# Moving six pairs' leftover gate/up rows into the attention stage of an adaLN transformer block, with a two-step layernorm

## The chip, the cores and the metric

The kernel is one launch on one core of a Trainium2 chip. It is measured in microseconds of device time for one execution; of several executions the median is given. TensorE (PE in the profile) multiplies matrices, PEld is its loading of stationary operands, VectorE (DVE), ScalarE (ACT) and GpSimd (POOL) work element by element, SyncE (SP) issues most of the DMAs. A profile is one execution that the hardware profiler recorded.

## The reference

An adaLN block in float32: x has 2 batches of 1024 tokens of width 1024. All matrices are dense.

```python
mod = (_silu(L0_c) @ L0_wmod).reshape(2, 6, 1, -1)
sa, ca, ga, sb, cb, gb = (mod[:, i] for i in range(6))
ga, gb = (sign * max(|g|, 0.25) for g in (ga, gb))
h = _layernorm(x) * (1 + ca) + sa
# attention: qkv = clip(h @ Wqkv.T); layernorm of q and of k over the width of 1024;
# 32 heads of 32, causal, ALiBi slopes, softmax, then the output product with Wout
x = x + ga * attention(h)
h = _layernorm(x) * (1 + cb) + sb
# gated MLP with 2752 inner rows
x = x + gb * (((_silu((h @ Wg.T) * ag) * ((h @ Wu.T) * au)) @ Wd.T) * ad)
```

## The kernel before

**Products.** Every large product is done by the Strassen-Winograd scheme: seven products of quarter operands in place of eight. `seven` runs them for 256 tokens (a *pair* of token tiles; `j` counts four pairs of each batch `b`) with two alternating PSUM banks x and y, four matmuls of 512 columns each; a float32 matmul shows as two records in the profile. `operand` builds the seven stationary operands of a pair from the attention's result, after it has fetched the reciprocals of the softmax sums (`rb`, spread over partitions) and multiplied them in (`aoA`).

**Order.** The stages are: modulation vectors; the q, k and v projections of batch 0; attention of batch 0 beside the projections of batch 1; attention of batch 1 beside the output products of six pairs (all four of batch 0, two of batch 1); a tail; the gate and up products of the FFN (line 1789, tiles gx, gy, ux, uy); the down product.

**Attention.** A unit is four heads (`k` counts eight groups), 512 queries and 128 keys: `scores` writes two PSUM tiles `sc`, each with one buffer; ScalarE writes exponentials into `p` (line 1056, 4 instructions of up to 512 columns; for k = 0 and 1 in pieces of 128 and 256 columns); GpSimd cuts the causal triangle; two units later `weigh` multiplies by v into `av`. Sums of `p` are added by VectorE and GpSimd and summed over keys by `settle`; `reciprocals` sends the sums of one (batch, 512 queries) through DRAM and back. TensorE's order is fixed as the program has it (`in_order`); other engines' orders are made by the framework from its own estimates, with each engine working in order.

**The dealing out.** `attention` and `dense_work` are generators that yield estimated microseconds. `together` advances the dense one until its sum reaches `share(a)`, where `a` is attention's sum. Each unit gives `unit_us` twice, once after its scores and once after its weighing. `DENSE0` and `DENSE1` are how much dense work is laid beside batch 0 and batch 1:

```python
def unit_us(b, qb, k, jb):
    return (0.2 + width(qb, jb) / 512) * SLOW[b].get(k, 1.0)
...
    return LEAD + DENSE0 + DENSE1 * max(a - att_us[0] - 8.0, 0.0) / (att_us[1] - 8.0)
```

**The output step of a pair** (`output`): seven products in chunks of two matmuls; `read` copies P1, U2 and P5 to SBUF (ScalarE) and adds the others to them (VectorE), multiplies by the gate and adds to the residual tile `xr` (GpSimd). Then the residual goes to DRAM, and `normalize` makes the second layernorm: statistics on VectorE, Ln and Exp on ScalarE, a correction and the product on VectorE. Four *turns* (four transposes each, evacuated by VectorE into `h2t`) follow as entries of a `Todo` list; `places` lets one entry run between chunks of the next pair. During attention a Todo entry has one spare PSUM bank (`banks.others`), which `settle` uses too.

**The rest rows.** The inner rows of the FFN are taken in five blocks of 512; 192 rows are left over. `rest_rows` computes them for a pair: three row products (gate rows, up rows, and 64 of each), each 8 matmuls of 256 columns (16 records `rest<-hl,restw`), then Silu on ScalarE, a product on VectorE and two DMA stores (`actr`). All eight pairs are done in the tail, as cover for other things there: `with_turns` lays rows beside turns, `between` lays them beside the output products of the last two pairs. Their weights (`rest_weights`, 1.5 MB) are loaded at the start of the tail. `fetch` brings h2 of a finished pair back (`hl`); `second` forms the Strassen combinations of both batches (`inner_b`, tiles `inner_T`, `oo`) and stores them (`bop`) for the FFN.

Of the kernel before, what the change touches and what calls it, by code (L numbers as in the profile page):

```python
# [12 lines left out]
FP = mybir.dt.float32  # L13
# [467 lines left out]
def kernel(  # L481
# [225 lines left out]

    def normalize(tiles, outs, small, nm):

# [8 lines left out]
        ve = small.tile([P, n], FP, tag="ve", name=f"ve_{nm}")  # L718
        nc.vector.tensor_scalar_add(ve, mv[:, :, 1], EPS)
        lv = small.tile([P, n], FP, tag="lv", name=f"lv_{nm}")  # L720
        nc.scalar.activation(lv, mv[:, :, 1], AF.Ln, bias=eps_t)
        rstd = small.tile([P, n], FP, tag="rstd", name=f"rstd_{nm}")
        nc.scalar.activation(rstd, lv, AF.Exp, scale=-0.5)
        fix = small.tile([P, n], FP, tag="fix", name=f"fix_{nm}")
        nc.vector.tensor_mul(fix, rstd, rstd)
        nc.vector.tensor_mul(fix, fix, ve)
        nc.vector.tensor_scalar(fix, fix, -0.5, 1.5, ALU.mult, ALU.add)
        nc.vector.tensor_mul(rstd, rstd, fix)
        for m, (t, o) in enumerate(zip(tiles, outs)):
            nc.vector.tensor_scalar(o, t, mv[:, m, 0:1], rstd[:, m : m + 1], ALU.subtract, ALU.mult)  # L730
# [5 lines left out]
    SLOW = ({0: 1.6, 1: 1.2}, {0: 2.6, 1: 1.4})  # L736
# [121 lines left out]
    class Todo:  # L858


        def __init__(self, banks):
            self.banks, self.list = banks, []
# [4 lines left out]
        def run(self, n, all_=False):  # L867
            for _ in range(min(n, len(self.list))):
                if not all_ and not self.banks.fresh():
                    return  # L870
                self.list.pop(0)(self.banks.turn())
                yield TURN

        def places(self, q0, n, side=lambda e: None):
# [3 lines left out]
            def between(q):  # L878
                side(order.index(q))
                if order.index(q) >= q0:  # L880
                    yield from self.run(n)
# [3 lines left out]
    def tokens(b, j, todo, ap_, xp, sm):  # L885
# [7 lines left out]
        normalize(xs, xs, sm, f"x{b}_{j}")  # L893
# [16 lines left out]
    def projections(b, pools, banks, places, extra=None, other=None, side=lambda n, e: None):  # L910
# [8 lines left out]
        for part in range(3):  # L919
            bt = weights_b(wp_, wqkv_t[:, ts(part, D)], f"{b}_{part}", wt_dram[part], other, b == 0 and part == 1)  # L920
            for j in range(NT // 2):
# [43 lines left out]
                normalize(raws, raws, sm, f"qk{b}_{part}_{j}")  # L965
# [15 lines left out]
    def behind(ins, first):  # L981

        tc.add_manual_dep(
            ins.ins, first.ins.name,
            mybir.DependencyInfo(mybir.DependencyClass.NoSync, mybir.DependencyReason.DATA),
            reason="behind",
        )

# [5 lines left out]
    def unit_us(b, qb, k, jb):  # L994
        return (0.2 + width(qb, jb) / 512) * SLOW[b].get(k, 1.0)
# [1021 lines left out]
```

## Time and profile before

| | us |
|---|---|
| three runs | 2932.33, 2937.59, 2945.91 |
| median | 2937.59 |
| the profiled execution | 2934.67 |
| its span, first to last instruction | 2932.9 |
| TensorE busy in it | 2728.3 |
| VectorE, ScalarE, GpSimd busy | 1436.5, 685.7, 1287.2 |
| attention of batch 1, first scores to last weighing | 989.4 to 1408.7 |
| first gate product of the FFN | 1585.45 |

Times in the profile count from the start of the span. A line of the timeline has the start, the length, the engine, the source line, the operation, what it writes and reads, and in brackets how long the engine had been idle and who released it. The granted clock of TensorE is a share of full speed. A line `L745` or `L748` is the helper that records all matmuls or transposes of the attention and output stages, so the tiles' names tell them apart.

### The profile page before, as it was taken

The page shows a single profiled execution, that of the slowest core. Times are in us where ns is not written, and L with a number is a line of the kernel's source. Part 1 is how long each engine was busy: PE and PEld are TensorE (multiplying, and loading weights), DVE is VectorE, ACT ScalarE, POOL GpSimd, SP SyncE. Part 2 cuts the span into 40 slices and gives each one's busy share as a digit, 9 for nine tenths or more (in the row PEclk, how much of TensorE's full clock was granted, in tenths as well). Part 3 has the DMA queues.
Part 4 walks back from the last instruction along what each step waited for, and adds up shares of the span by engine and source line. Part 5 has one row for each costly group of instructions (what it writes and reads, how often), then busy time and mean ns, then how long its engine had stood idle before and what let it go on. Part 6 is the DMA issues. An engine that isn't in the chain of part 4 may idle for free. (4 is left out here: it accounts for less than half of the span.)

```text
span 2932.9 us, 29881 instructions
## 1 busy us (share of the span) xinstructions
PE 2728.3 (93%) x10271; PEld 1335.4 (46%) x10271; DVE 1436.5 (49%) x2285; ACT 685.7 (23%) x1523; POOL 1287.2 (44%) x1270
## 2 busy tenths in 40 slices
PE   6999997899999888888799999999999998999998
PEld 2444332333333222222456444444444446888776
DVE  5666522466553455655554444453534446434442
ACT  1322242354434455555111011010101100000000
POOL 3312145434353655555456546463644641222343
PEclk9999998999999989999899999999999999999999
DMA  9867787463642654432578658575765759554542
GB/s 339 301 253 286 291 276 234 146 215 109 223 146 77 211 155 157 141 107 96 159 232 275 223 172 287 159 273 180 241 217 173 256 154 300 153 163 136 163 144 80
DMA packets 377571, 579.12 MB, mean 197 GB/s; under 512 B 21590, under 2 KB 278712, under 8 KB 366276
## 3 DMA queue, kind: packets, MB, share of 16 engines
q1 hardware_dynamic: 359768, 554.54, 58.1%
q10 hardware_dynamic: 17644, 22.59, 2.4%
q8 instruction: 84, 1.38, 0.2%
q14 instruction: 75, 0.61, 0.1%
HBM read 411.89 MB, written 165.17 MB: 197 GB/s over the span
## 5 line engine op out<-in xcount | busy, mean ns | idle before, releaser
L1056 ACT ACTIVATE p<-sc,kw 128x128 f32<-128x128 f32 (+3 forms) x1024 | 421.4, 513 | 356.6 <-PE sc L745 337.5
L745 PE MATMUL bank<-wT,a 128*128 128x512 f32 x768 | 361.5, 614 | 14.0 <-DVE raw L951 7.2
L1088 POOL TENSOR_TENSOR p<-p,p 128x1024 f32<-128x1024 f32 (+3 forms) x128 | 262.7, 2052 | 237.9 <-PE av L745 210.6
L1088 DVE TENSOR_TENSOR p<-p,p 128x1024 f32<-128x1024 f32 (+3 forms) x192 | 242.3, 1274 | 186.8 <-POOL p L1060 143.4
L745 PE MATMUL bank<-wB,a 128*128 128x512 f32 x576 | 265.9, 606 | 1.7 <-DVE raw L949 1.3
L745 PE MATMUL sc<-cq,ck 32*128 32x512 f32 (+3 forms) x1536 | 199.7, 558 | 69.2 <-ACT p L1056 68.8
L745 PEld LDWEIGHTS bank<-wT,a 128*128 128x128 f32 x768 | 142.6, 195 | 202.1 <-issue 181.0
L1060 POOL TENSOR_SCALAR_AFFINE_SELECT p<-p 128x256 f32<-128x256 f32 x256 | 136.4, 545 | 144.1 <-ACT p L1056 141.7
L745 PE MATMUL av<-p,cv 128*32 128x512 f32 (+3 forms) x1536 | 173.7, 515 | 20.7 <-POOL p L1060 20.7
L745 PEld LDWEIGHTS bank<-wB,a 128*128 128x128 f32 x576 | 105.2, 191 | 147.7 <-issue 129.1
L745 PEld LDWEIGHTS sc<-cq,ck 32*128 32x128 f32 x1536 | 66.8, 191 | 203.3 <-ACT p L1056 119.9
L1789 PE MATMUL gy<-bt,sig 128*128 128x512 f32 x280 | 132.5, 595 | 10.4 <-DMA bt<-bop_B 5.6
L1789 PE MATMUL gx<-bt,sig 128*128 128x512 f32 x280 | 131.6, 592 | 0.0
L1789 PE MATMUL ux<-bt,siu 128*128 128x512 f32 x280 | 131.6, 592 | 0.0
L1789 PE MATMUL uy<-bt,siu 128*128 128x512 f32 x280 | 131.6, 592 | 0.0
L745 PEld LDWEIGHTS av<-p,cv 128*32 128x32 f32 x1536 | 33.9, 110 | 139.7 <-issue 84.9
L951 DVE TENSOR_TENSOR raw<-P,bank 128x512 f32<-128x512 f32 x48 | 32.8, 684 | 125.3 <-PE bank L745 116.8
L1789 PEld LDWEIGHTS gy<-bt,sig 128*128 128x128 f32 x280 | 52.4, 190 | 80.8 <-issue 71.0
L1789 PEld LDWEIGHTS uy<-bt,siu 128*128 128x128 f32 x280 | 53.2, 190 | 67.0 <-issue 65.8
L1789 PEld LDWEIGHTS ux<-bt,siu 128*128 128x128 f32 x280 | 53.2, 190 | 67.0 <-issue 65.1
L1789 PEld LDWEIGHTS gx<-bt,sig 128*128 128x128 f32 x280 | 53.2, 190 | 67.0 <-issue 65.9
L745 PE MATMUL rest<-hl,restw 128*128 128x256 f32 x288 | 67.0, 391 | 14.9 <-DVE xn L730 14.9
(416 smaller groups left out, 4500.1 us busy)
## 6 DMA issues: line engine op xcount, KB each, us to landing
bt<-bop_T SPq DMA_DIRECT2D x140, 512.0 KB
bt<-bop_B SPq DMA_DIRECT2D x99, 512.0 KB
a<-hop SPq DMA_DIRECT2D x20, 1792.0 KB
wm<-in_L_wmod_dram SPq DMA_DIRECT2D x48, 512.0 KB
wB<-in_L_attn_Wqkv_dram SPq DMA_DIRECT2D x21, 1024.0 KB
aq_S<-act_S SPq DMA_DIRECT2D x16, 1280.0 KB
qk<-qs SPq DMA_DIRECT2D x16, 1024.0 KB
act_S<-asS SPq DMA_DIRECT2D x30, 512.0 KB
```

The source lines that it names most:

```text
L745: return in_order(nc.tensor.matmul(*args, **kw_))
L951: nc.vector.tensor_add(dst, part_t[MATE[q]], bank)
L1056: nc.scalar.activation(p[:, g, lo:hi], sp[:, g, lo:hi], AF.Exp, bias=kw[:, d, h_ : h_ + 1])
L1060: nc.gpsimd.affine_select(out=p[:, :, 0:P], in_=p[:, :, 0:P], pattern=[[0, 2], [1, P]], compare_op=ALU.is_ge, fill=0.0, base=0, channel_mu ...
L1088: adders[b](half, jb).tensor_add(dst, dst, ps[half][:, :, 0:n])
L1789: nc.tensor.matmul(ps.rearrange("p (j t) -> p j t", j=NJ), ins[mat][qa][:, c2, :], bt[:, :, c2, :], start=(q in ("P1", "P2", "P5") and c2 ...
```

## The change

**Rest rows.** `rest_rows` is replaced by `rest_piece`, one row product as a Todo entry. `output` adds three of them after the turns of each pair while attention runs, so six pairs (all of batch 0 and two of batch 1) have their rows dealt out beside attention. Their weights are loaded when the output stage begins. Silu is written as x times the reciprocal of 1 + exp(-x): Identity and Exp on ScalarE, minimum, reciprocal and product on VectorE. Pairs 2 and 3 of batch 1 keep their rows in the tail.

**Layernorm.** `normalize` makes the statistics at once and returns the rest as a function. For the projections of batch 1 and the output steps up to pair 0 of batch 1 it is run at the first place of the next step (`Todo.first`, `Todo.place`); elsewhere at once. The Ln is put behind the last exponential recorded before it.

**Dealing out.** `unit_us` is half of an estimate of the exponentials' time less a part for the products; `DENSE1` goes from 136 to 205.

**The tail.** Both operands of the last two pairs are made at once (one in its own pool); the tail's fetches go to SP's queue; the output products of the last two pairs run without rows between them. `xr` has two buffers instead of four, and the sums are kept in the copies' tiles.

```diff
-    SLOW = ({0: 1.6, 1: 1.2}, {0: 2.6, 1: 1.4})
     def unit_us(b, qb, k, jb):
-        return (0.2 + width(qb, jb) / 512) * SLOW[b].get(k, 1.0)
+        n, span, end = width(qb, jb), SPAN.get(k, QB), (qb + 1) * QB
+        y0 = end - n
+        parts = [y + span - max(y, y0) for y in range(y0 // span * span, end, span)]
+        return 0.5 * (0.4 + sum(1.2 + 4 * 0.39 * w / 512 for w in parts) - (0.25 + 0.8 * n / 512))
-    LEAD, DENSE0, DENSE1 = 16.0, 370.0, 136.0
+    LEAD, DENSE0, DENSE1 = 16.0, 370.0, 205.0
     def normalize(tiles, outs, small, nm):
...
+        def rest_():
...
+            ln = nc.scalar.activation(lv, mv[:, :, 1], AF.Ln, bias=eps_t)
+            if last_exp[0] is not None:
+                behind(ln, last_exp[0])
...
+        return rest_
     class Todo:
...
+        def first(self, go, now):
+            if now:
+                go()
+            else:
+                assert self.due is None
+                self.due = go
+        def place(self):
+            if self.due is not None:
+                self.due()
+                self.due = None
         def run(self, n, all_=False):
+            self.place()
             for _ in range(min(n, len(self.list))):
                 if not all_ and not self.banks.fresh():
                     return
-                self.list.pop(0)(self.banks.turn())
-                yield TURN
+                more = self.list.pop(0)(self.banks.turn())
+                if more is None:
+                    yield TURN
+                else:
+                    yield from more
     def projections(...)
-                normalize(raws, raws, sm, f"qk{b}_{part}_{j}")
+                todo.first(normalize(raws, raws, sm, f"qk{b}_{part}_{j}"), b == 0)
     def output(...)
-            normalize(xs, xn, sm, f"f{b}_{j}")
+            todo.first(normalize(xs, xn, sm, f"f{b}_{j}"), b == 1 and j >= NJ // 2 - 1)
...
+            if rest is not None:
+                for r in range(3):
+                    todo.add(rest_piece(b, j, r, *rest))
+    def rest_piece(b, j, r, rest_w, pool):
...
+        def go(bank):
+            hl = kept[b, j].rearrange("p k h t -> p k (h t)")
+            ps = bank[:, 0:256]
+            for k in range(KC):
+                matmul(ps, rest_w[r][:, k, :], hl[:, k, :], start=(k == 0), stop=(k == KC - 1))
+            if r != 1:
+                g, e = tile_("rg", r), tile_("re", r)
+                nc.scalar.activation(g[hi], ps[lo], AF.Identity, scale=ag_)
+                nc.scalar.activation(e[hi], g[hi], AF.Exp, scale=-1.0)
+                nc.vector.tensor_scalar(e[hi], e[hi], FAR, 1.0, ALU.min, ALU.add)
+                nc.vector.reciprocal(e[hi], e[hi])
+                nc.vector.tensor_mul(g[hi], g[hi], e[hi])
+                sig[b, j, gate] = g
+            if r != 0:
+                ac = tile_("rac", r)
+                nc.vector.scalar_tensor_tensor(ac[hi], ps[hi], au_, sig[b, j, gate][hi], ALU.mult, ALU.mult)
+                nc.sync.dma_start(
+                    rest_dram[gate][0 : n1 if gate else P, b, j], ac[hi].rearrange("p (h t) -> p h t", h=2)
+                )
+            yield 3.5
+        return go
     # output stage
-            for n, k in (("oga", 1), ("tok", 4), ("opart", 1), ("osmall", 2), ("ao", 1))
+            for n, k in (("oga", 1), ("tok", 2), ("opart", 1), ("osmall", 2), ("ao", 1))
+        rest = rest_weights(rwp, nc.sync), rwp
     # tail
-    fetch(0, 0, nc.scalar)
-    rest_w = rest_weights(rest_pool, nc.scalar)
-    fetch(1, 0, nc.scalar)
-    made = {(1, NJ // 2): operand(1, NJ // 2, opools[1])}
-    fetch(0, 1)
-    with_turns(rows((0, 0), (1, 0)))
-    fetch(1, 1)
-    def between():
-        yield from rows((0, 1))
-        second(0)
-        yield from rows((1, 1))
-    together(
-        between(), output(1, range(NJ // 2, NJ), *out_args, made, 3), lambda a: 0.6 * OUT_US / 2 * a / 20.6
-    )
+    made = {(1, NJ // 2): operand(1, NJ // 2, opools[1], wide)}
+    made[1, NJ // 2 + 1] = operand(1, NJ // 2 + 1, opools[1])
+    fetch(0, 0)
+    fetch(1, 0)
+    alone(todo.run(len(todo.list), True))
+    fetch(0, 1)
+    fetch(1, 1)
+    second(0)
+    alone(output(1, range(NJ // 2, NJ), *out_args[:-1], None, made, 3))
     in_range(rest_pool, rps)
+    second(1)
     fetch(0, 2)
-    second(1)
     fetch(0, 3)
-    with_turns(rows((0, 2), (1, 2)))
+    with_turns(rows(2))
     second(2)
-    alone(rows((0, 3), (1, 3)))
+    alone(rows(3))
```

## Prediction before the result

> **What bounds the kernel now.** I read the page's slices first, then the windows by stage, then the waits and the timeline around the change.
>
> ```profile
> PE   6999997899999888888799999999999998999998
> ACT  1322242354434455555111011010101100000000
> PEclk9999998999999989999899999999999999999999
> ```
>
> A slice is 73 us. TensorE (PE) is busy almost everywhere; the weak stretch is slices 13 to 19, attention of the second batch (8 tenths, where ScalarE is at 4 to 5) and the end of it. Nothing here is bound by ScalarE's sum of work. The windows, with the borders I took from the attention's tiles, give it in microseconds (columns: stretch, length, busy time of PE, its weight loads, VectorE, ScalarE, GpSimd, then granted clock, DMA share, GB/s):
>
> ```profile
> 600.00:800.00 200.00, 197.52 (x917) 74.70 (x916) 124.86 (x217) 90.74 (x233) 80.81 (x60) 1.00 0.51 177
> 989.00:1410.00 421.00, 350.62 (x2026) 113.04 (x2024) 232.87 (x343) 227.89 (x553) 242.50 (x231) 0.91 0.40 124
> 1410.00:1425.00 15.00, 14.05 (x40) 5.92 (x40) 5.85 (x11) 1.02 (x2) 4.90 (x5) 1.00 0.80 271
> 1425.00:1440.00 15.00, 0.25 (x1) 0.00 (x0) 7.12 (x19) 0.86 (x3) 5.39 (x4) 0.62 0.81 239
> 1440.00:1540.00 100.00, 96.10 (x337) 62.66 (x338) 56.44 (x99) 12.43 (x20) 47.26 (x41) 0.97 0.72 210
> 1540.00:1585.00 45.00, 43.32 (x208) 37.55 (x207) 24.23 (x52) 8.45 (x12) 18.06 (x18) 1.00 0.83 283
> 1585.00:1634.00 49.00, 46.45 (x109) 20.22 (x108) 21.23 (x30) 5.62 (x10) 46.02 (x63) 1.00 0.77 244
> ```
>
> Attention of batch 0 (600 to 800) leaves PE no gap. Attention of batch 1 (989 to 1410) leaves 70.4 us idle in 421, and runs at a mean clock of 0.91. Then 15 us finish the dealt-out output products, 15 us are empty, and from 1440 on the tail is full. So there is room before 1410 and none after 1440: that is what this change trades on. Who makes the 70 us (waits, 989 to 1410):
>
> ```profile
> PE sc L745 <- ACT p L1056: 55.1, 43, 7.1
> ACT lv_f L721 <- DVE mv_f L717: 28.5, 4, 8.9
> PE bank L748 <- DVE h2t L851: 9.4, 2, 7.6
> ```
>
> Scores wait for the exponentials that still read the one score buffer. Some exponentials are late only because a layernorm's Ln stands in front of them in ScalarE's order and waits for VectorE's statistics. The timeline shows it: scores at 1264.20, Ln at 1272.37, the exponentials right behind it, the next scores after 6.16 us of idle PE.
>
> ```profile
> 1264.20 0.71 PE L745 MATMUL sc<-cq,ck 32*128 32x256 f32 x8
> 1272.37 0.30 ACT L721 ACTIVATE lv_f<-mv_f,eps_t 128x2 f32<-128x2 f32 x1 [8.90 <-DVE mv_f L717]
> 1272.57 1.55 ACT L1056 ACTIVATE p<-sc,kw 128x256 f32<-128x256 f32 x4
> 1274.17 0.81 PE L745 MATMUL sc<-cq,ck 32*128 32x128 f32 x8 [6.16 <-ACT p L1056]
> ```
>
> The end of attention, and what the rows cost:
>
> ```profile
> 1431.17 0.32 SPq L1218 DMA_DIRECT2D rb<-rec  x1
> 1434.66 3.37 ACTq L1342 DMA_DIRECT2D restw<-in_L_ffn_Wg_dram  x1
> 1440.13 13.36 PE L745 MATMUL rest<-hl,restw 128*128 128x256 f32 x48 [14.89 <-DVE xn L730]
> 1448.23 1.27 POOL L1233 TENSOR_TENSOR aoA<-aoA,rb 128x512 f32<-128x512 f32 x1 [12.34 <-DMA rb<-rec]
> 1563.83 10.53 PE L745 MATMUL rest<-hl,restw 128*128 128x256 f32 x48
> 1585.45 1.88 PE L1789 MATMUL gx<-bt,wgA 128*128 128x512 f32 x4
> ```
>
> 48 records of one pair take 10.4 us warm, so one of its three row products is 3.45 us.
>
> **The tail.** From 1425 to the first FFN product at 1585.45 are 160.4 us. PE's work in it: 24 row products x 3.45 = 82.8; two output steps, 112 records x 0.43 (3.60 us for eight with their ramp) = 48.2; twelve turns (0.60 each plus about 0.3 until the evacuation) = 10.8; sum 141.8; so 18.6 are waits, 14.9 of them the gap before 1440.
> The change moves 15 row products into attention; the three of pair (1,1) stay behind it as the last of the list, six more belong to the last two pairs. PE's work falls by 51.8 to 90. The cover falls with it, so the waits must be counted anew:
> - Operand of the third pair. Last weighing 1408.72, sum stored 1413.36, read back 1420.64, reciprocal 1424.08, stored 1425.06, fetched from 1431.17, product with it at 1448.23: 39.5 us. The legs to 1431 stay. The last leg, 17.1 us, shared the DMA with 1.5 MB of row weights, which now come long before; bounds are 3.4 us (the reload at 1420.64) and 17.1, and I take 9, since 2 MB of `hl` still travel. With the multiply that is T+33, T being the last weighing. PE has the settling, four turns and three row products until T+17: 16 us idle (10 to 24).
> - Last normalization: 1540.1 to 1550.2 now, less two table loads of 1.28, so 7.5; the first row product hides 3.45: 4 us. The last turn's evacuation before `rows(3)`: 2 us.
> - Combinations (`second`): without rows between them VectorE's `inner` writes stand in front of evacuations of the two output steps, and can wait for a store (6.83 us seen at 1569); two banks give 3.4 us of slack. 0 to 14, I take 5.
> Sum 90 + 16 + 4 + 2 + 5 = 117, against 160.4: 43 us less. On SP's queue the moved steps cost nothing that I count: the actr stores (two a pair) now go out during attention (DMA share 0.40). With two buffers instead of four an xr load waits for the normalization that moved one product later, and chunk loads stand behind it; but chunks are fetched two groups, some 30 us, ahead, and the first product that needs xr ends about 16 us into its step. Were that cover gone, each of six steps would lose up to the 10 us of a normalization.
>
> The trace's own row for that fetch (17.1 us with row weights issued from ScalarE's queue) already says that another queue did not shield it. The Trainium skill, DMA: Bandwidth & Descriptors, section Issuing engines are not separate DMA queues, gives the rule: all queues share the same 16 engines and interleave. By the rule the fetches moved from ScalarE's queue to SP gain nothing by that, and only the earlier time of the row weights can; a sum with no gain on this leg would leave 8 us more idle.
>
> **Attention of batch 1.** Before, dealt work was out at 1425: 350.6 busy + 70.4 idle + 15 after = 436 us from 989. After:
> - Busy: 350.6 + 14.0 (the work of 1410 to 1425) + 15 x 3.45 = 416.4.
> - Clock: four records took 3.78 us at 1206.26 against 1.98 elsewhere. Scores and weighing of batch 1 sum to 195.5 us, of batch 0, the same products at clock near 1, to 178.0; 270 output records cost 0.526 each against 0.470 there. All of it is 32 us; denser work recovers a part, I take 10 (0 to 32).
> - Idle of layernorm: longest waits of 7.6, 7.1, 6.2 and 3.8, in all 24.7. The Ln is now put behind the last exponential and one product later; its statistics are ready by then (3 us of GpSimd, 0.9 us of VectorE against a step of some 4 us). 4 remain (0 to 15).
> - Other idle, 45.7: short gaps of a microsecond between units. `unit_us` now gives a full unit 2 x 1.06 x 205/234 = 1.85 us of dense work, one chunk of four records, and a 128-wide unit 1.35 (0.51 before), so gaps of narrow units are filled; a row product of 3.45 is too long for one gap. 27 remain (15 to 46).
> - New: the row products use the only spare bank. It is held through Identity and Exp (0.47 each, as the Silu of this shape), on VectorE min-add and product (0.44 each, by `inner` of this shape), reciprocal (0.94 for 128 wide, so 1.87) and the last product 0.48: 4.2 us, up to 7 behind an addition of 1.5 and its neighbour. Until the next taker PE has a chunk and a unit's products, 4 us. So 0 to 3 us for ten of fifteen, 0 to 30; I take 8. PE being in order, scores stand behind it. VectorE's 32 us more (5 x 6.4) on 233 of 421 and ScalarE's 9.4 on 228 are hidden.
> Sum 416.4 - 10 + 4 + 27 + 8 = 445, so T = 1434: 9 us later. Bounds: -26 (unlikely all together) and +70.
>
> The clock term by a page: the Trainium skill, TensorE: Matmul & The Clock Gate, section What's actually happening, halves the clock after an idle window of about 3.4 us and restores it after as long a busy one. This speaks against the tail of the change: its 16 us gap starts the third output step cold, an estimated 1.7 us by that page, which I leave out of the sum.
>
> **Batch 0** is full of PE work; its eight normalizations delay ScalarE by 2.7 to 5.5 us each without PE showing it, while the Ln one product later can make a turn wait. I take 0 (-8 to +8).
>
> **Transfers.** DMA share times length from 1410 to 1634 is 171 us. Without row weights and with what now falls into attention some 150 remain, in about 167 us: 0.9 of full use, near the best stretches (0.83). I add 4.
>
> Sum: -43 + 9 + 0 + 4 = -30. The profiled execution took 2934.67 (span 2932.9), so 2904.7; the median lies 2.9 above it: **2908**.
>
> **Rivals.**
> 1. Better: clock recovers wholly and rows fit the gaps; T 15 earlier than 1425: 2880. For it: batch 0 with as many dense records holds 1.00. Against: gaps are short. 0.15.
> 2. Transfers bind the tail: if 0.8 is all it can hold, 150 us of transfers need 188, 20 more than I allow: 2926. For it: 6.8 to 14.7 us waits on stores after 1550. Against: 0.83 over 45 us. 0.15.
> 3. Slower, by the one spare bank: each of ten row products makes PE wait 3 us (30), no gap is filled (46), the clock stays: 416.4 + 30 + 46 + 4 = 496, T 60 later, net +21: 2959. Without the bank it is a shift of 30; it turns slower by over 0.5% once the wait passes 2.4 us each. For it: VectorE's queue holds additions of 0.9 to 1.5 us. Against: at least a chunk stands between. 0.18.
> That the rows are not dealt out in time is covered by the third: they would then drain behind attention, uncovered.
>
> **Numbers.** 0.5% (14.7 us) is about what a measurement of this kernel can tell from no change. My case has 0.52 and its own range of 2886 to 2926. Faster: 0.52 and 0.15, less an edge, 0.66; same 0.17; slower 0.17. The range reaches over the first rival's price and to the third's: 2872 to 2958.
>
> **What would show it.** Right: last weighing near 1434, clock above 0.95 and PE idle near 40 in batch 1; no Ln wait over 3 us there; an idle stretch of 10 to 24 us before output step (1,2); first gx about 117 us after the last weighing. Wrong: PE waiting for VectorE before row products (rival 3), or for bt or gate weights at the first FFN products (rival 2).

## The result and the profile after

The changed kernel takes 2970.84 us (median of four runs, 2965.85 to 2978.29) against 2939.15 for the kernel before, run beside it: a ratio of 1.011, interval 1.0078 to 1.0142. It is slower by some 32 us, where 31 less were forecast. Its profiled execution took 2970.97 us (span 2969.2) against 2934.67 (span 2932.9). The stages, by positions in the two timelines:

| stage, us | before | after | difference | forecast |
|---|---|---|---|---|
| up to the first scores of batch 1 | 989.4 | 985.1 | -4 | 0 |
| from there until the dealt-out work is done | 435.6 (to 1425) | 485.7 (to 1470.8) | +50 | +9 |
| from there to the first gate product | 160.4 | 124.5 | -36 | -43 |
| from there to the FFN's second group (first `gx<-bt,wgS`) | 51.4 | 77.6 | +26 | 0 (and 4 for transfers) |
| the rest | 1296.1 | 1296.3 | 0 | 0 |

The slices of the page after, as they were shown of before:

```profile
PE   7999897999997898888876899999999998999998
ACT  1322143344443445445300101010110101000000
PEclk9999999999998899999888999999999999999999
```

Counted from 0 as in the prediction, slices 13 to 18 of PE (attention of batch 1) are about as weak as before. Slices 19 to 21 (the end of attention, the tail and the FFN's first products) stand at 7, 6 and 8 tenths, where it was 7, 9 and 9, and the granted clock dips in the same three. The windows, same columns as before (stretch, length, busy time of PE, weight loads, VectorE, ScalarE, GpSimd, clock, DMA share, GB/s; 1497 to 1510 is left out):

```profile
985.10:1471.00 485.90, 418.32 (x2306) 162.60 (x2306) 297.64 (x405) 238.81 (x576) 242.50 (x237) 0.92 0.38 116
1471.00:1497.00 26.00, 14.13 (x64) 11.99 (x63) 22.43 (x43) 1.77 (x4) 4.81 (x2) 0.76 0.91 261
1510.00:1595.00 85.00, 62.19 (x185) 35.85 (x184) 54.48 (x99) 5.58 (x13) 47.80 (x42) 0.86 0.79 266
1595.00:1673.00 78.00, 61.26 (x148) 29.32 (x147) 53.26 (x54) 9.14 (x15) 59.56 (x77) 0.89 0.65 208
```

The last three rows are the tail and the FFN's first group, at a clock of 0.76 to 0.89 where it was 0.97 to 1.00 from 1440 on before. The first row is the one to read longest. PE's busy time rose by 54 us over the 364.3 of before (15 row products of 3.45 are 51.8; the three of pair (1,1) run behind it), and 67.6 us are still idle, against 71.3 before. The row work did not go into the idle time; it was added to it. The waits of PE from 985 to 1468 say who released it (columns: who waited for whom, sum, times, longest). `rac` is the result of a row product, `xn` the normalized residual, `h2t` its transpose:

```profile
PE sc L762 <- ACT p L1087: 26.6, 21, 3.8
PE bank L762 <- DVE rac L1408: 13.0, 2, 8.0
PE bank L765 <- DVE xn L746: 11.6, 4, 4.2
PE bank L765 <- DVE h2t L868: 6.8, 2, 4.1
```

The waits of scores for exponentials halved (55.1 before), and waits for VectorE took their place. The longest wait on `rac`, with lines of all engines in the order of time (a selection):

```profile
1435.14 0.47 ACT L1400 ACTIVATE rg<-bank,vt 64x256 f32<-64x256 f32 x1 [2.89 <-PE bank L762]
1436.09 0.29 DVE L1402 TENSOR_SCALAR re<-re 64x256 f32<-64x256 f32 x1 [7.00 <-ACT re L1401]
1436.30 2.34 POOL L1119 TENSOR_TENSOR p<-p,p 128x1024 f32<-128x1024 f32 x1 [7.94 <-PE av L762]
1436.41 3.32 DVE L1119 TENSOR_TENSOR p<-p,p 128x1024 f32<-128x1024 f32 x1
1439.76 1.75 DVE L1403 RECIPROCAL re<-re 64x256 f32<-64x256 f32 x1
1441.54 1.22 DVE L1119 TENSOR_TENSOR p<-p,p 128x1024 f32<-128x1024 f32 x1
1442.79 0.42 DVE L1404 TENSOR_TENSOR rg<-rg,re 64x256 f32<-64x256 f32 x1
1443.25 1.22 DVE L1119 TENSOR_TENSOR p<-p,p 128x1024 f32<-128x1024 f32 x1
1444.50 0.49 DVE L1408 SCALAR_TENSOR_TENSOR rac<-bank,vt,rg 64x256 f32<-64x256 f32 x1
1445.14 1.94 PE L762 MATMUL bank<-p,ones 128*32 128x512 f32 x8 [7.97 <-DVE rac L1408]
```

VectorE puts an addition of attention between every two links of the sigmoid chain. The chain's own links, with the Exp between the first two lines (0.41), sum to 3.8 us, and the one spare bank is held for 10; the settling of a head group (`p,ones`), which needs that bank, waits 7.97. The addition that ran beside GpSimd's took 3.32 us, alone 1.22. The Trainium skill, "SBUF — State Buffer", section Who interferes with whom, says that a VectorE instruction with two SBUF inputs shares a port with a GpSimd instruction that reads SBUF; 1.22 and 2.34 one after the other would be 3.56, so this trace agrees.

The gaps of the tail in PE's timeline (in brackets the idle time and its end):

```profile
1497.64 9.15 PE L762 MATMUL bank<-wB_o,aoA 128*128 128x512 f32 x16 [12.04 <-DMA actr<-rac]
1538.95 7.27 PE L762 MATMUL bank<-wT_o,aoS 128*128 128x512 f32 x12 [8.13 <-ACT oP L1299]
1571.49 1.12 PE L765 MATMUL bank<-ident,xn 128*128 128x128 f32 x4 [7.93 <-DVE xn L746]
1589.75 5.77 PE L762 MATMUL rest<-h2t,restw 128*128 128x256 f32 x16 [6.76 <-DVE h2t L868]
1623.65 3.78 PE L1829 MATMUL gy<-bt,sig 128*128 128x512 f32 x4 [7.62 <-DVE gX L1638]
1656.17 3.78 PE L1829 MATMUL gy<-bt,sig 128*128 128x512 f32 x4 [8.62 <-DVE gC L1638]
```

Six gaps of 7 to 12 us, each with a different owner, two of them already in the FFN (`oP` is the copy of a product's bank, `gX` and `gC` are sums of gate products). The first names the store of a row's result, but VectorE's last part of the operand (`aoA`) ended at 1497.43, 0.2 us before the product; I count that gap to the operand. The records behind each gap are slow: the first 16 above took 9.15 us, the 16 at 1506.63 took 7.03.

### The profile page after: what moved, and what is told of

It is laid out like the page before. It is cut to its first block, busy times and chain, and to the rows that moved or that the text cites. A ratio compares the mean times of both kernels' runs of the same rounds, so it can differ in the third digit from the quotient of the medians.

```text
span 2969.2 us, 29944 instructions
## 1 busy us (share of the span) xinstructions
PE 2740.1 (92%) x10271; PEld 1340.4 (45%) x10271; DVE 1521.2 (51%) x2333; ACT 683.3 (23%) x1532; POOL 1279.5 (43%) x1270
## 4 chain that ended last, share of the span: by engine, by line
PE 62%; DVE 6%; DMA 5%; issue 4%; POOL 3%; ACT 2%; SPq 1%; POOLq 0%; DVEq 0%; ACTq 0%
PE bank L762 15%; PE ux L1829 7%; PE gx L1829 7%; PE dx L1954 7%; PE gy L1829 6%; PE uy L1829 5%; PE dy L1954 5%; PE sc L762 4%; PE av L762 3%; ACT p L1087 2%; DMA bt<-bop_B 2%; DVE p L1119 1%; PE bank L765 1%; POOL xr L1309 1%; DVE inner_T L1196 1%
## 5 line engine op out<-in xcount | busy, mean ns | idle before, releaser
L1119 POOL TENSOR_TENSOR p<-p,p 128x1024 f32<-128x1024 f32 (+3 forms) x128 | 254.3, 1987 | 230.3 <-PE av L762 181.9
L762 PE MATMUL sc<-cq,ck 32*128 32x512 f32 (+3 forms) x1536 | 187.9, 544 | 34.3 <-ACT p L1087 34.1
L1091 POOL TENSOR_SCALAR_AFFINE_SELECT p<-p 128x256 f32<-128x256 f32 x256 | 128.8, 516 | 158.4 <-ACT p L1087 153.6
L762 PE MATMUL av<-p,cv 128*32 128x512 f32 (+3 forms) x1536 | 173.1, 515 | 14.9 <-POOL p L1091 14.9
L762 PE MATMUL bank<-wB_o,aoA 128*128 128x512 f32 x128 | 71.2, 693 | 27.7 <-DVE aoS L1265 15.7
L1829 PE MATMUL gx<-bt,wgS 128*128 128x512 f32 x160 | 75.2, 592 | 0.0
```

Of the source, the lines that this page charges most:

```text
L762: return in_order(nc.tensor.matmul(*args, **kw_))
L1091: nc.gpsimd.affine_select(out=p[:, :, 0:P], in_=p[:, :, 0:P], pattern=[[0, 2], [1, P]], compare_op=ALU.is_ge, fill=0.0, base=0, channel_mu ...
L1119: adders[b](half, jb).tensor_add(dst, dst, ps[half][:, :, 0:n])
L1829: nc.tensor.matmul(ps.rearrange("p (j t) -> p j t", j=NJ), ins[mat][qa][:, c2, :], bt[:, :, c2, :], start=(q in ("P1", "P2", "P5") and c2 ...
```

## Experiments

Theories at the start. For attention: **full price** (PE works in order, its idle time is no room), **chain** (VectorE's chain in the one bank costs on top), **deferral** (the layernorm one product later makes turns wait). For the tail: **cover** (the rows filled gaps of other chains there and cost little). The positions below are from each run's profiled execution, the medians from 4 to 10 runs (of the kernel before 4 to 14). Kernels whose attention is the same, differing only in the tail or the rooms (changed kernel, single operand, swap), had attention stages of 482.9, 476.5 and 475.8 us in their one profile, so a difference of 7 us between two such stages is not read as an effect.

| run | first scores b. 1 | last weighing | first gx | FFN 2nd group | median, us | ratio to before |
|---|---|---|---|---|---|---|
| before | 989.4 | 1409.5 | 1585.4 | 1636.9 | 2937 to 2940 | |
| changed | 985.1 | 1468.0 | 1595.4 | 1673.0 | 2970.84 | 1.011 |
| e1 changed, no rows, 205 dealt | 993.3 | 1426.8 | 1550.7 | 1625.6 | 2924.61 | 0.9953 |
| e2 before, no rows of six | 993.4 | 1414.0 | 1578.2 | 1636.4 | 2932.72 | 0.9982 |
| e3 no sigmoid | 986.7 | 1446.9 | 1585.4 | 1650.7 | 2955.23 | 1.0062 |
| e4 layernorm at once | 986.6 | 1461.4 | 1588.7 | 1665.8 | 2958.75 | 1.0067 |
| e5 copied out of the bank | 981.8 | 1451.1 | 1588.0 | 1652.9 | 2957.76 | 1.0067 |
| e6 new rows in the tail | 988.0 | 1399.9 | 1575.6 | 1667.2 | 2966.89 | 1.0101 |
| e7 the same, layernorm at once | 978.3 | 1390.6 | 1566.8 | 1659.8 | 2961.84 | 1.0081 |
| e8 old pace | 1007.9 | 1479.2 | 1609.4 | 1676.3 | 2980.72 | 1.0144 |
| e9 old rows in the tail | 985.1 | 1397.1 | 1560.6 | 1612.4 | 2914.14 | 0.9917 |
| e10 the same, layernorm at once | 980.4 | 1396.3 | 1562.4 | 1613.5 | 2913.55 | 0.991 |
| e11 rows mended | 981.4 | 1449.1 | 1583.1 | 1651.4 | 2957.08 | 1.0065 |
| e12 single operand | 984.3 | 1460.8 | 1599.4 | 1661.6 | 2964.55 | 1.009 |
| e13 changed, no rows, 136 dealt | 990.7 | 1389.3 | 1526.4 | 1590.9 | 2890.82 | 0.9835 |
| e14 e9, old pace | 1011.0 | 1425.3 | 1589.7 | 1641.4 | 2940.15 | 1.0002 |
| e15 e9, single operand | 984.4 | 1402.2 | 1566.5 | 1617.4 | 2914.73 | 0.9904 |
| e16 before, new pace | 969.8 | 1391.5 | 1568.3 | 1619.6 | 2917.37 | 0.992 |
| e17 e9, pools swapped | 980.0 | 1392.2 | 1556.0 | 1610.3 | 2910.6 | 0.991 |
| e18 changed, pools swapped | 980.3 | 1456.1 | 1583.1 | 1656.6 | 2961.73 | 1.0093 |

### What the rows cost where they stand

**e1**, the rows left out beside attention:

```diff
-                for r in range(3):
-                    todo.add(rest_piece(b, j, r, *rest))
+                todo.add(bare)        # the two stores alone, from h2
```

> The changed kernel with the row work of its six pairs left out of the list beside attention (15 row products of 3.45 us and their Silu chains; only stores of the same size are kept, from the tile of the layernorm). It gives the price of the rows in attention. Changed kernel: last weighing at 1467.4 us, total 2971; before: 1408.7 and 2935 to 2939. Absorbed (what the prediction said, most of the product falls into idle time): last weighing only 15 to 25 us earlier, total 2945 to 2955. Full price (PE is in order and nothing is absorbed): 45 to 55 us earlier, total about 2920. Chain (the one spare bank, held by the row's VectorE chain, makes PE wait on top of the products): 65 to 80 us earlier, total 2890 to 2905.

46 us less than the changed kernel, last weighing 41 earlier: it looked like full price. It was not a clean price, since 205 us were still dealt from a list that is some 60 us shorter (18 entries of 3.5 us, the list's own estimate, are gone). The windows of its last 150 us of attention show the list running out:

```profile
1293.30:1343.30 50.00, 42.19 (x257) 13.17 (x256) 32.09 (x40) 27.80 (x56) 30.42 (x26) 0.95 0.26 89
1343.30:1393.30 50.00, 35.62 (x248) 8.59 (x240) 27.15 (x22) 32.18 (x61) 26.78 (x20) 0.88 0.25 85
1393.30:1443.30 50.00, 28.36 (x208) 8.37 (x208) 29.66 (x38) 20.82 (x43) 24.92 (x22) 0.80 0.27 95
```

**e13** mends that:

```diff
 (e1, and)
-    LEAD, DENSE0, DENSE1 = 16.0, 370.0, 205.0
+    LEAD, DENSE0, DENSE1 = 16.0, 370.0, 136.0
```

> The changed kernel without its rows of six pairs (as in the first run: only stores of the same size are kept), but dealing 136 us of work over the second batch in place of 205, so that the list does not run out before attention ends. It is the clean price of the rows. With the rows in the tail in their old form the time was 2914. If rows in the tail are nearly free (5 us, as in the kernel before): 2905 to 2912, last weighing near 1397. If they cost 20 or more even there: below 2895. If the pace was not what held the first run at 2924: within 5 us of 2924.

2890.82, the second expectation's case: 23 us less than with the rows in the tail in their old form (2914.14 in e9, below), and 80 less than with them beside attention. Against e1 it is 34 us less, by the dealt number alone. So the same work costs 80 us in its new form and place. The run leaves out 18 products: in the changed kernel 15 of them take 57.5 us of PE beside attention (3.83 each) and the last three 10.6 behind it, 68 in all. The stage from the first scores to the end of the dealt-out work:

```profile
990.70:1405.10 414.40, 354.77 (x2065) 116.92 (x2064) 242.42 (x357) 229.14 (x554) 251.72 (x235) 0.94 0.46 139
```

Beside the changed kernel's 485.9 with 418.3 busy, it is 71 us shorter with 64 us less work: PE's idle time is 59.6 here and 67.6 with the rows. None of the added work went into it, on balance.

**e2**, the same from the other end, in the kernel before:

```diff
     for b, j in pairs:
+        if b == 0 or j < 2:
+            ...               # the two stores alone
+            continue
```

> The kernel before with the row work of six of the eight pairs left out of its tail (18 row products, 62 us of PE by the prediction's 3.45; stores of the same size are kept), rows of the last two pairs kept. It gives the price of the rows where they stood. If the tail is PE's sum, the total falls by 60 or more, to 2873 or less. If the rows were cover for chains of operand, normalization and transfers (which then show as gaps), the fall is 20 to 35 us: 2903 to 2918, and PE gaps of 8 us and more appear before output step (1,2), the first gx and in the FFN's second stage.

Only 5 us less (ratio 0.9982, 0.9971 to 0.9993), far below even the cover theory's 20 to 35: 62 us of PE work (18 products) had cost next to nothing. What they had covered now shows in PE's timeline:

```profile
1447.57 1.11 PE L748 MATMUL bank<-ident,xn 128*128 128x128 f32 x4 [17.84 <-DVE xn L730]
1506.76 9.60 PE L745 MATMUL bank<-wB_o,aoA 128*128 128x512 f32 x16 [21.43 <-DVE aoA L1233]
1553.01 1.11 PE L748 MATMUL bank<-ident,xn 128*128 128x128 f32 x4 [6.15 <-DVE xn L730]
1620.28 3.78 PE L1793 MATMUL gy<-bt,sig 128*128 128x512 f32 x4 [7.62 <-DVE gC L1602]
```

The tail before looked full because it had been filled. (In the changed kernel the old rows cost 23 us, by e9 and e13. That is not all a price of the tail: the two attention stages, without rows in either, differ by 12 us, and e13 keeps the last two pairs in the new form.)

### Form of the rows, and repairs beside attention

**e3**, the sigmoid left out:

```diff
-                nc.scalar.activation(e[hi], g[hi], AF.Exp, scale=-1.0)
-                nc.vector.tensor_scalar(e[hi], e[hi], FAR, 1.0, ALU.min, ALU.add)
-                nc.vector.reciprocal(e[hi], e[hi])
-                nc.vector.tensor_mul(g[hi], g[hi], e[hi])
```

> The changed kernel without the sigmoid of its rows (Exp, min-add, reciprocal, product left out; Identity, the last product and the store stay). VectorE's chain behind a row's first product shortens from some 4 us to none. If the chain in the one spare bank is the loss: waits of PE on rac (13.0 us) go, last weighing 13 to 25 us earlier, total 2945 to 2958. If the row's PE time and its place are the loss: within 5 us of 1467 and of 2971.

15.6 us less, attention 460 in place of 483, the clock in it 0.95 in place of 0.92 (PE's busy time 406.1 in place of 415.8 for the same products), and 54 us idle in place of 67. The chain costs, but not most of it.

**e5**, the bank freed at once:

```diff
+            if r != 0:
+                ac = tile_("rac", r)
+                nc.scalar.activation(ac[hi], ps[hi], AF.Identity, scale=au_)
...
-                nc.vector.scalar_tensor_tensor(ac[hi], ps[hi], au_, sig[b, j, gate][hi], ALU.mult, ALU.mult)
+                nc.vector.tensor_mul(ac[hi], ac[hi], sig[b, j, gate][hi])
```

> The changed kernel with one edit: the half of a row product that is multiplied up is copied out of the bank by ScalarE (Identity with its scale, 10 more in the list) at once, and VectorE's last product reads the copy. The sigmoid chain stays on VectorE. So the bank is no longer held through VectorE's chain. If holding the bank is what the sigmoid costs (15.6 us of the total, 20 us of attention when it was left out): waits of PE on rac (13.0 us) go, last weighing at 1446 to 1455 against 1467, total 2953 to 2960. If VectorE's time is (its 33 us of row work delay turns, masks and evacuations): within 5 us of 2971.

13.1 us less, last weighing at 1451, and of the 13.0 us of waits on `rac` 1.2 are left (on ScalarE's copy). VectorE still has the chain, so holding the bank looks like most of what the sigmoid cost: 13.1 of 15.6 us, and 13.6 of the 22.7 by which e3 shortened attention.

**e4**, `True` in place of the two conditions of `todo.first`:

```diff
-                todo.first(normalize(...), b == 0)
+                todo.first(normalize(...), True)
```

> The changed kernel with every layernorm of the list done at once, as before, in place of one product later. If the deferred step makes the turns wait (11.6 us of waits on xn, 11.1 on h2t in batch 1): last weighing 10 to 20 us earlier than 1467, total 2952 to 2962. If it does what it is for: the waits of Ln return (24.7 us before), scores wait for exponentials again, last weighing 5 to 20 us later, total 2976 to 2990.

12.1 us less. ScalarE's waits of Ln came back (25.0 us), and PE's waits of scores for exponentials rose by only 3.7 (26.6 to 30.3): hardly any of those Ln waits were PE's.

**e11**, all three together, the chain on ScalarE:

```diff
 (e4 and e5, and)
-                nc.vector.tensor_scalar(e[hi], e[hi], FAR, 1.0, ALU.min, ALU.add)
-                nc.vector.reciprocal(e[hi], e[hi])
+                nc.scalar.activation(e[hi], e[hi], AF.Ln, bias=1.0)
+                nc.scalar.activation(e[hi], e[hi], AF.Exp, scale=-1.0)
```

> The changed kernel with rows beside attention, mended by what the runs showed: multiplied half copied out of the bank at once, the reciprocal's chain moved to ScalarE (Ln and Exp), layernorm at once. If the losses by sigmoid (16), bank (13) and deferral (12) add as far as they are different things: last weighing 1435 to 1445, total 2938 to 2946. If ScalarE's 2 x 0.42 us more a chain delay exponentials: 2950 to 2960. If it falls below 2930, rows beside attention pay after all.

2957.08: the repairs do not add. Each of them brought 12 to 16 and all of them 14. Part of each may be the kind of shift that unrelated edits gave here (6 us in e12, 9 in e18). What no repair touches is this line, beside that of the changed kernel above:

```profile
981.40:1450.00 468.60, 401.73 (x2298) 158.20 (x2298) 271.30 (x380) 250.68 (x606) 250.64 (x237) 0.95 0.39 119
```

PE is idle for 66.9 us, as in the changed kernel (67.6) and as in e9, which has no rows here (66.2). The row products go on top.

### The rows back in the tail

**e6**, new pieces, old place (`DENSE1` 136 again; the main lines of the edit):

```diff
-        yield from output(0, range(NJ), *out_args, made)
+        yield from output(0, range(NJ), *out_args[:-1], None, made)
...
+    with_turns(rows((0, 0), (1, 0)))
+    together(between(), output(1, range(NJ // 2, NJ), ...), lambda a: 0.6 * OUT_US / 2 * a / 20.6)
+    with_turns(rows((0, 2), (1, 2)))
```

> The changed kernel with the rows of all six pairs put back where they stood, between and beside the last output steps (same pieces and sigmoid chain; dealt work 136 again); operands at once, layernorm in two steps and the new pace stay. The runs so far say that the rows cost 5 us in the tail and 46 beside attention; by that: last weighing near 1425, first gx some 165 to 176 us after it, total 2925 to 2935, at or just below the kernel before. If the rest of the change is what costs: total 2950 or more. If operands at once save their wait in the tail even with rows there (the prediction's third term): 2915 to 2925.

A surprise: last weighing at 1400, and yet 2966.89, in the second expectation's range but not for its reason. All of it was lost again in the tail, and one line of PE's waits from 1410 to 1690 says to what:

```profile
PE rest L762 <- DVE rac L1408: 39.6, 6, 23.3
```

The pieces have one buffer each for `rg`, `re` and `rac`; `rac` waits for its store (up to 18.9 us on `actr<-rac` in the list of waits), and the product that needs the bank behind it waits in turn. So this run does not give the price of the place alone, and the old form beside attention was not run either.

**e7**, the same with the layernorm at once:

```diff
 (e6, and in both calls of todo.first)
+                todo.first(normalize(...), True)
```

> As the run with the rows put back, and every layernorm at once. With the rows beside attention this gave 12 us. If the deferral costs by turns that wait for xn, the gain stays: 8 to 14 us below the run with rows put back. If it cost only because rows filled the same bank: within 4 us of it; if its Ln waits (25 us on ScalarE) bind when nothing else does: 5 to 15 us above.

5 us less, between two of the expectations; with e10 below it is no proof of either.

**e9**, the old `rest_rows` with Silu and four banks, in the old place:

```diff
 (e6, and)
-            for r in range(3):
-                yield from rest_piece(b, j, r, *rest)(...)
+        return rest_rows(pairs, rest[0], rest_pool, rps, kept)
-    rps = rest_st.enter_context(tc.tile_pool(name="rest_ps", bufs=2, space=PSUM))
+    rps = rest_st.enter_context(tc.tile_pool(name="rest_ps", bufs=4, space=PSUM))
-    banks.others = banks.others + [...]      # two more banks for the turns
```

> The changed kernel with the rows of six pairs back in the tail in their old form (three banks of four a pair, Silu of ScalarE straight from the bank, no sigmoid chain, no single buffer), dealt work 136; new pace, deferred layernorm and operands at once stay. In the run with the rows put back in the new form PE waited 39.6 us on rac in the tail. If the form is what costs there: total 2915 to 2930, last weighing near 1400, no wait on rac. If rows cost in the shortened tail whatever their form, since operands at once already filled its gaps: 2945 to 2965.

2914.14, faster than before by 0.8% (0.9901 to 0.9934). The form of the rows (Silu straight from the bank, four banks, one result tile a pair) is worth 53 us in the tail, against e6; form and place together are worth 57 against the changed kernel. Its attention and its tail:

```profile
985.00:1411.00 426.00, 359.84 (x2065) 117.90 (x2065) 245.56 (x356) 229.36 (x554) 255.31 (x236) 0.94 0.43 130
1440.00:1540.00 100.00, 92.00 (x324) 58.27 (x324) 50.83 (x106) 17.04 (x25) 45.07 (x38) 0.98 0.82 270
1560.60:1612.40 51.80, 48.92 (x114) 21.07 (x113) 23.67 (x33) 5.89 (x11) 48.56 (x67) 1.00 0.78 250
```

Attention has 66.2 us idle with 52 us less work in it, and the tail is full at clock 0.98 to 1.00, the FFN's first group included.

**e10**, e9 with the layernorm at once:

```diff
 (e9, and in both calls of todo.first)
+                todo.first(normalize(...), True)
```

> As the run with the rows in the tail in their old form, and every layernorm at once. If the deferral costs without rows beside attention too: 3 to 10 us below that run. If it pays there as the prediction had it (24.7 us of Ln waits): 5 to 15 us above.

The same time within 1 us. The two-step layernorm is worth nothing either way once the rows are gone.

### What the rest of the change is worth

**e8** and **e14**, the old `unit_us` and `SLOW` in the changed kernel and in e9:

```diff
-        return 0.5 * (0.4 + sum(1.2 + 4 * 0.39 * w / 512 for w in parts) - (0.25 + 0.8 * n / 512))
+        return (0.2 + width(qb, jb) / 512) * SLOW[b].get(k, 1.0)
```

> The changed kernel with the old estimate of a unit's time (width, and fixed factors for the heads in four or two exponentials), the dealt sum of 205 us kept. If dealing by the exponentials' time fills gaps of narrow units (prediction: 18 us of idle): last weighing 10 to 20 us later than 1467, total 2980 to 2990, waits of scores on exponentials up from 26.6 us towards 45. If the pace is no cause either way: within 5 us of 2971. If it costs, by putting row products at narrow units whose VectorE chain is longest: total 2955 to 2965.

> The run with the rows in the tail in their old form (2914), with the old estimate of a unit's time. Its attention of the second batch was 10 us shorter than before. If that is the pace's: 2922 to 2932, dealt work of batch 1 done 8 to 15 us later. If it is the deferred layernorm's or noise: within 5 us of 2914.

Slower by 10 and 26 us. But the place is not the expected one: the first scores of batch 1 come 23 and 26 us later, and their attention is no longer than with the new pace (471 against 483, 414 against 412). The new pace works in batch 0.

**e16**, the new `unit_us` alone in the kernel before:

```diff
-        return (0.2 + width(qb, jb) / 512) * SLOW[b].get(k, 1.0)
+        ...               # n, span, end, y0 and parts as in the change
+        return 0.5 * (0.4 + sum(1.2 + 4 * 0.39 * w / 512 for w in parts) - (0.25 + 0.8 * n / 512))
```

> The kernel before with the new estimate of a unit's time alone. If the pace gives what the first batches show by themselves: 2924 to 2934, 5 to 14 us below before. If it needs the deferral or the freed rooms of the change: within 5 us of 2937.

2917.37, 22 us less than before (0.9904 to 0.9937), more than expected. The window from 350 to 650 of the kernel before shows where (columns as above):

```profile
350.00:650.00 300.00, 266.33 (x1161) 103.08 (x1158) 125.26 (x219) 109.31 (x306) 141.36 (x185) 0.95 0.69 225
```

and the same window of e16:

```profile
350.00:650.00 300.00, 281.16 (x1209) 109.89 (x1207) 140.21 (x245) 110.52 (x309) 141.88 (x185) 0.97 0.71 237
```

PE had 33.7 us idle there, in the first units of batch 0 (scores from 379), and the new pace fills 15 of them.

**e12** and **e15**, the last operand made in its own step again, with four `xr` buffers in the room, in the changed kernel and in e9:

```diff
-    made = {(1, NJ // 2): operand(1, NJ // 2, opools[1], wide)}
-    made[1, NJ // 2 + 1] = operand(1, NJ // 2 + 1, opools[1])
+    made = {(1, NJ // 2): operand(1, NJ // 2, opools[1])}
```

> The changed kernel with the last operand made in its own step again (one buffer each), and the room of the operands at once given to four xr buffers of the tail's two steps, so that x is loaded at once. Last weighing stays at 1467. If the wait for xr (ACT oP behind POOL xr, 24 us; PE 8.1) is the larger loss: first gx 5 to 10 us sooner than 127 after the last weighing, total 2961 to 2966. If operands at once are what shortened the tail: a gap of 15 to 21 us before output step (1,3) comes back, as in the kernel before without its rows, total 2980 to 2992.

> The run with the rows in the tail in their old form (2914), with the last operand made in its own step again and four xr buffers in the tail. Its tail was 11 us shorter than before. If operands at once shortened it (the 14.9 us gap of the kernel before has gone): 2920 to 2930. If the table loads, the early row weights and the lighter transfers did: within 5 us of 2914.

6 us less, and 0.6 more. In e12 the first gx came 138.6 us after the last weighing (127 before the edit), so the gain is not where the expectation had it, and its size is one that an unrelated edit gave too: inconclusive. In its tail PE's wait of 8.1 us for `oP` is gone, but a gap of 15.8 us before output step (1,3) has come, the second expectation's sign. In e15, with rows as cover, operands at once are worth nothing. The kernels that load the row weights before the tail (e9, e10, e14, e15, e17) take 215 to 218 us from the last weighing to the FFN's second group, those that load them in it (before, e16) 227 to 228; that fits the gap of 14.9 us before the first row product in the kernel before, but no run isolates it.

**e17** and **e18**, two pools in the other order, in e9 and in the changed kernel:

```diff
-            for n, k in (("oga", 1), ("tok", 2), ("opart", 1), ("osmall", 2), ("ao", 1))
+            for n, k in (("oga", 1), ("tok", 2), ("opart", 1), ("osmall", 2), ("restw", 1), ("ao", 1))
```

The reason for them is a wait of PE that the kernel before does not have (its list from 380 to 985, after):

```profile
PE bank L762 <- DVE aoS L1265: 15.7, 1, 15.7
```

and the fetch of the first output step's operand, in SP's timeline of the kernel before:

```profile
837.59 1.92 SPq L1218 DMA_DIRECT2D rb<-rec  x4
```

and of the changed kernel, 94 us later:

```profile
931.50 0.33 SPq L1249 DMA_DIRECT2D rb<-rec  x1
```

> The run with the rows in the tail in their old form (2914), with two memory pools in the other order: the row weights' pool stands before the operand's. In the changed kernel the first output step's operand shares its room with tiles of the last projection, is fetched from 931 (837 before) and its first product waits 15.5 us at about 953. With the pools swapped the fetch is free again. If that wait is a loss of its own: first scores of the second batch near 970 (985 there), total 2896 to 2903. If the row weights, now late, bring 1.5 MB into that stretch instead: within 5 us of 2914.

> The changed kernel with the same two pools swapped and nothing else. If the losses add: first scores of the second batch near 970, total 2954 to 2960, so still slower than before by 0.6% with rows beside attention. If what batch 0 gives is taken by the waits of batch 1: 2966 to 2974.

With the swap the fetch goes out at 812 and 784 and the wait on `aoS` is gone in both, so the rooms were its cause. In its place PE waits 8.4 us at the same product for `wB_o`, now behind the late row weights; half is won. The medians fall by 3.5 and 9 us. e17, 2910.6 us (0.991, 0.9893 to 0.9926), is the fastest kernel here that does all the work; it stands within a few us of e9 and e10.

## Why the prediction was wrong

**The account.** From the runs: pace -22 (e16; -26 by e14), rows in new form and place +57 (changed against e9), two-step layernorm and operands at once about 0 beside it (e10, e15). Together +31 to +35, against 32 measured. With e14's figure the sum closes by construction, since e14 itself takes the time of the kernel before (1.0002); the check is e16, where the pace alone, in another kernel, gives nearly the same.

**Attention: the step "other idle" (45.7, of which 27 were to remain) failed, and with it the sum.** Busy 416.4 was right (418.3), and so was the forecast that scores would wait less (26.6 in place of 55.1). But of 71.3 us idle 39 were to remain (4 + 27 + 8); 67.6 remained. The clock term failed with it: 10 us were to come back at over 0.95, and at 0.92 none did. I treated idle time as room. Over the twenty kernels, with 355 to 418 us of work from the first scores to the end of the dealt-out work, idle time was 55 to 77 us, and more work did not make it less: 59.6 without rows (e13), 67.6 with them. The lowest with rows are the runs that ease the chain (54.9 in e3, 60.7 in e5). Why the short gaps persist when more is dealt is not isolated; that a row product is longer than a gap fits it and was not tested.

**"Idle of layernorm: 24.7 to 4" was no gain.** ScalarE's Ln waits did go (28.5 to 3.1), but in e4 and e10, with the layernorm at once, the kernel is as fast or faster: PE did not have them to lose. The waits were read from PE's gaps that lay next to an Ln; that the one made the other was inferred from one place in the timeline.

**The one spare bank: 8 was too little.** The waits on `rac` are 13.0 and e5 gained 13 (though e4, which leaves the bank alone, gained 12). Rival 3 came nearest: no gap filled, the clock as before, attention 60 us longer (50 measured); I gave it 0.18. Its price of the bank, 30, was too high, and its total of 2959 too low, since it kept the -43 of the tail.

**Tail: the step "combinations (`second`), I take 5" failed.** PE's work until the first gx was put at 90; it is 91.2 from 1468 to 1595. Operand 12.0 (16 forecast), last norm 7.9 (4), last turn 6.8 (2; VectorE stood before it in a combination that waited 6.8 us for `hl`). Where the combinations had 5, there are 8.1 for P1's tile, held until GpSimd's addition to `xr`: GpSimd was in combinations from 1524.0 to 1535.9 and then waited 0.9 us more for `xr`, whose load went out only at 1531.35, with two buffers; in e12, with four, this wait is gone. Together 34.8 in place of 27, so the first gx came 8 us later than forecast. The larger part lay behind it: 26 us in the FFN's first group. Two row products stand there (7.1 in all) and gaps of 7.6 and 8.6. Before the first gap's end VectorE waited 5.6 us for the store of a row's result. Before the second the chain that ended last runs through one combination on VectorE:

```profile
1641.33 13.52 DVE inner_T L1196
```

The same instruction took 0.41 us at 1488.00, and 4.13 at this place in the kernel before. It ended 0.3 us after GpSimd's unbroken run of weight combinations (1627.3 to 1654.6), both with two inputs in SBUF, as in the pair of additions above; that the one held the other fits and was not tested. My sum ended at the first gx and so saw none of this. e9 has the same `second` with two pairs' rows behind it, 20.7 us of PE, and takes 51.8 for this group; without rows as cover the kernel before takes 58.2 (e2), and without the sigmoid the changed one 65.3 (e3). So cover and sigmoid each have a part, and no run here gives their sizes by themselves.

**The clock after a gap.** The 16 records behind the 12.04 us gap took 9.15 us, the same 16 in e9 without a gap 7.03: 2.1 us. From the Trainium skill, "TensorE: Matmul & The Clock Gate", section What's actually happening, the prediction had estimated 1.7 us for this cold start, and left it out of the sum; the trace is 0.4 us above that.

**Batch 0: 0 was right by luck, through two errors that cancel.** -20 by the pace (e16) and +16 by the operand's wait made -4. "Batch 0 is full of PE work" rested on the window from 600 to 800; the one from 350 to 650 would have shown 33.7 us idle.

**Transfers** were not the bound that rival 2 meant: DMA share is 0.65 to 0.91 in the tail after, and no gap of PE there waits for bt. Single transfers (`hl`, `xr`, a row's store) do stand behind gaps, as links in a chain; the chain into the last one runs through loads of bt (1622.8 to 1636.7) and a store to `bop_B` (to 1641.3) before VectorE's combination.

## What to carry to other kernels

A stage that looks full may be full of filler: before moving work out of it, ask what the stage's other chains take without that work. e2 is the test: leave the work out and see whether the time falls. Idle time of an in-order engine beside short dependent steps is no room until a run shows it shrinking. And look at every stretch that a planner governs, not at one window: here the part of the change that paid worked in a stage that the forecast had put at zero.

## What was not expected of the hardware

An addition of 128x1024 on VectorE took 1.22 us by itself and 3.32 beside one of GpSimd; in a chain that holds a PSUM bank, such an addition between two links lengthened the hold by as much. A subtraction of 128x256 on VectorE, 0.4 us elsewhere, took 13.52 during a run of GpSimd without a break. The reciprocal of 256 columns took 1.75 us where the product of the same shape took 0.42.
